# A graph network in four layers: where the turned rows are copied, and when, in layer 3

## The chip, the cores and the metric

The kernel runs on one core of a Trainium2 chip. Its time is what the device takes for one execution, in microseconds (us); a measured time is a median of several executions. Beside it one execution was profiled. The core's engines are named as in the profile: PE (TensorE, matrix products), PEld (its weight loads), DVE (VectorE), ACT (ScalarE), POOL (GpSimd) and SP (SyncE, which here only issues transfers).

## What is computed

A graph of 3327 nodes has 256 features per node (`x`) and a dense adjacency matrix `adj` of 0 and 1. Four layers follow each other, and each ends in `x = layernorm(x + layer(x, adj))`. Layer 0 is an attention by cosine similarity, layer 1 a graph attention, layer 2 an attention with queries, keys and values. Layer 3, which the change concerns, is three graph attentions in a row:

```python
def _gat_layer(h, adj, W, a):
    Wh = h @ W
    f1 = Wh @ a[:F_out]
    f2 = Wh @ a[F_out:]
    e = leaky_relu(f1 + f2.T, 0.01)
    att = softmax(where(adj > 0, e, -9e15), axis=1)
    return elu(att @ Wh)

h = x @ W0
h = _gat_layer(h, adj, W1, a1)
h = _gat_layer(h, adj, W2, a2)
h = _gat_layer(h, adj, W3, a3)
```

All is in 32-bit floating point. The kernel applies a sublayer's attention to its input first and multiplies by `W` afterwards; `W0` is folded into `W1`.

## The kernel before

**Tiles, blocks and steps.** The nodes are padded to 26 tiles of 128 (`NT`). Destination nodes go in 7 blocks (`NB`): blocks 0 to 5 have 512 nodes, block 6 has 256. The main loop (L1552) runs over six sublayers (keys "0", "1", "2", "3a", "3b", "3c"), inside each over the blocks `b`, and inside each block over the 26 source tiles `j`. One turn of the innermost loop is called a step here.

**Weights.** For each step a tile of unnormalised attention weights is needed, 128 source nodes by the 512 nodes of the block. In layer 3, ACT makes `re` from a row of scores `u` (L787; four buffers, tag "a"), and DVE turns `re` into `ft` with the adjacency mask (L800). The main loop asks for the weights several steps ahead of their use (`ahead_of`, L1573 to 1581).

**Products.** Two source tiles and two halves of the block make a 2x2 product by Strassen's method in Winograd's form. DVE builds the sums of weights `qsum` (L871 to 874), four tiles at a time. The sums of the other operand, `tsums`, were stored in memory by `combine` (L830) in the sublayer before and are fetched by SP (L857), one for each pair of steps, into three buffers. `products` (L907) issues 14 products for each pair of steps, so 182 for a block; the trace has two records for each product, since a 32-bit product is done in two passes. Accumulation is in four banks of PSUM, of five.

**The finish of a block.** When a block's last step is done, `finish` (L1093) is started for it. It is a generator, and `advance` (L1457) runs it on to its next `yield` once per step, so its parts are spread over the steps of the next block. At step 22 all that is left of it is run out (L1691). For a block of layer 3 the parts are these:

1. `joined` (L943) on DVE adds the partial products up; `normed` on ACT divides by the row sums and gives `p4`.
2. `turn` (L983): ACT splits the 32-bit numbers of `p4` into 16-bit halves (`planes`, L990, two copies of 128x1024). SP issues a transposing DMA from `planes` to `turned` (L993). After `steps` yields, two copies of 128x1024 (L1000), on DVE, put the halves together as `pT`, the turned rows.
3. `projected(k)` for each of four tiles: two products on PE with `W` (L1230, four passes, to `pproj`), then an exponential on ACT (`elu_e`, L1239) and either a second activation on ACT (`z`, L1242, in 3a and 3b) or an operation of DVE (L1245, in 3c).
4. `activated(k)`, one yield after `projected(k)`: DVE makes the new row (L1254). In 3a and 3b it adds it to a running sum (L1084) and makes the scores for the next sublayer (L719); `combine` follows after the second and the fourth tile. In 3c, statistics, normalisation (L1283) and the output DMAs follow.
5. In 3a and 3b, after three more yields, `rows` (L761): a transposition of the scores on PE (`psr`, L765), a copy on ACT (L767) and a small DMA.

How many steps the DMA is given is set by `turn_steps`; `b == NB - 2` is block 5, whose finish runs in the short block 6:

```python
if L.key == "1":
    return 5 if b == NB - 2 else 3
return (9 if L.key == "3c" else 7) if b == NB - 2 else 4
```

**Order.** The loop gives each operation a place, and buffers give it its waits. The order in which the instructions stand on each engine in the trace is not simply that of the loop: DVE's `joined` is mixed with `qsum`, for example. A planner at build time decides it from the loop's order and from when it thinks inputs are ready.

The buffers of the finish: `planes`, `pT` and `combine`'s `tsum` share the tag "x4k" (two buffers), `p4`, `turned` and 3c's `x4` and `o4` the tag "stage" (four), projections the three PSUM banks of `bank`.

Of the kernel before, what the change touches and what calls it, by code (L numbers as in the profile page):

```python
# [33 lines left out]
def gnn_stack(ctx: ExitStack, tc: tile.TileContext, a: dict, N: int, out: bass.AP):  # L34
# [8 lines left out]
    nc = tc.nc  # L43
    NT = (N + P - 1) // P
    NP = NT * P
    NB = (NP + CH - 1) // CH
# [36 lines left out]
    n = 8  # L83
# [738 lines left out]
    def deep(L):  # L822
        return L.i > 2
# [6 lines left out]
    def combine(key, p, v, e=None):  # L830


        b1, b2 = v[2 * p], v[2 * p + 1]
        b11, b12, b21, b22 = b1[:, H:D], b1[:, :H], b2[:, H:D], b2[:, :H]
        if (key, p) in kept or key == "0":
            t = work.tile([P, 4 * H + 1], F32, tag="tsum", name="tsums", bufs=3)
        else:
            t = work.tile([P, 4 * H + 1], F32, tag="x4k", name="tsum", bufs=2)
        if (key, p) in kept:
            tsums[kept[key, p], p] = t  # L840
        t1, t2, t3, t4 = (t[:, c : c + H] for c in (0, H + 1, 2 * H + 1, 3 * H + 1))
        if e is None:
            nc.gpsimd.memset(t[:, H : H + 1], 1.0)
            nc.vector.tensor_tensor(t1, b12, b11, ALU.subtract)
            nc.vector.tensor_tensor(t3, b22, b12, ALU.subtract)
        else:
            one = t[:, H : H + 1]
            nc.vector.tensor_scalar(one, e[:, :1], 0.0, None, ALU.is_ge)
            nc.vector.scalar_tensor_tensor(t1, b12, one, b11, ALU.mult, ALU.subtract)
            nc.vector.scalar_tensor_tensor(t3, b22, one, b12, ALU.mult, ALU.subtract)  # L850
        nc.vector.tensor_tensor(t2, b22, t1, ALU.subtract)
        nc.vector.tensor_tensor(t4, t2, b21, ALU.subtract)
        nc.sync.dma_start(t_d[key][p], t)
# [126 lines left out]
        return z[:, : 2 * q]  # L980


    def turn(x4, n, out, steps=3):  # L983

        half = "p k (n t) -> p t k n"
        pl = work.tile([P, 4, 2, D], U16, tag="x4k", name="planes", bufs=2)
        for t in range(2):
            nc.scalar.copy(pl[:, :n, t, :], x4[:, :n, :].bitcast(U16).rearrange(half, t=2)[:, t])  # L990
        yield
        tr = work.tile([P, 16, P], U16, tag="stage", name="turned", bufs=4)
        nc.sync.dma_start_transpose(  # L993
            out=tr[:, : 4 * n, :], in_=pl[:, :n].rearrange("p k t n -> p (k t n)")
        )
        for _ in range(steps):
            yield
        trv = tr[:, : 4 * n, :].rearrange("p (k t h) i -> p t k h i", t=2, h=2)
        for t in range(2):
            nc.vector.tensor_copy(out(t), trv[:, t])  # L1000
        yield

    def turn_steps(L, b):

        if L.key == "1":
            return 5 if b == NB - 2 else 3
        return (9 if L.key == "3c" else 7) if b == NB - 2 else 4

# [82 lines left out]
    def finish(L, b, pos):  # L1093
# [4 lines left out]
        n = len(ts_)  # L1098
# [71 lines left out]
        else:  # L1170
# [23 lines left out]
            if L.key in x_d:  # L1194
                x4 = work.tile([P, 4, D], F32, tag="stage", name="x4", bufs=4)
# [8 lines left out]
            if L.key != "2":  # L1204
                pT4 = work.tile([P, 4, 2, P], F32, tag="x4k", name="pT4", bufs=2)
                yield from turn(
                    p4,
                    n,
                    lambda t: pT4[:, :n].bitcast(U16).rearrange(
                        "p k h (i t) -> p t k h i", t=2  # L1210
                    )[:, t],
                    turn_steps(L, b),
                )
                pTs = {k: pT4[:, k] for k in range(n)}
                if L.key == "1" and b < NB - 2:
                    c4 = work.tile([P, 4, D], F32, tag="x4k", name="c4", bufs=2)
                    yield from projected4(pT4, w[L.w], c4)

            def projected(k):


                if L.key == "2":
                    src = p4[:, k, :]
                elif L.key == "1" and b < NB - 2:
                    src = c4[:, k, :]
                else:
                    pm = bank("pproj")
                    pT = pTs.pop(k)
                    for h in range(2):
                        nc.tensor.matmul(  # L1230
                            pm[:, :D],
                            pT[:, h, :],
                            w[L.w][:, h, :],
                            start=(h == 0),
                            stop=(h == 1),
                        )
                    src = pm[:, :D]
                e = work.tile([P, D], F32, tag="elu_e", name="elu_e", bufs=2)
                nc.scalar.activation(e, src, AF.Exp)  # L1239
                if L.hidden:  # L1240
                    y = work.tile([P, D], F32, tag="y", name="z", bufs=6)
                    nc.scalar.activation(y, src, AF.Relu)  # L1242
                else:
                    y = work.tile([P, D], F32, tag="y", name="y", bufs=6)
                    nc.vector.scalar_tensor_tensor(  # L1245
                        y, src, 0.0, xr[k], ALU.max, ALU.add
                    )
                es[k] = e
                ys.append(y)

            def activated(k):
                e, y = es.pop(k), ys[k]
                x = nxt[ts_[k]][:, :D] if L.hidden else y
                nc.vector.scalar_tensor_tensor(x, e, 1.0, y, ALU.min, ALU.add)  # L1254
                if L.hidden:
                    follow([k], {k: x})
                else:
                    stats(k)

            for p in range(n + 2):  # L1260
                if p >= 2:
                    activated(p - 2)
                    if b == NB - 2:
                        yield
                    if L.hidden and p % 2 and b < NB - 1:
                        combine(layers[L.i + 1].key, (ts_[0] + p - 3) // 2, nxt)
                if 1 <= p <= n:
                    projected(p - 1)
                if p > 0:
                    yield  # L1270
        if not L.hidden:
# [29 lines left out]
            if L.key == "1":  # L1301
                yield from turn(
                    o4,
                    n,
                    lambda t: FT[b].bitcast(U16).rearrange(
                        "p h (k i t) -> p t k h i", k=4, t=2
                    )[:, t, :n],
                    4 if b == NB - 2 else 3,
                )
                for k, t in enumerate(ts_):  # L1310
                    pm = bank("pv")
                    for h in range(2):
                        nc.tensor.matmul(
                            pm[:, :D],
                            FT[b][:, h, k * P : (k + 1) * P],
                            w["v"][:, h, :],
                            start=(h == 0),
                            stop=(h == 1),
                        )
                    nc.vector.tensor_tensor(nxt[t][:, :D], pm[:, :D], w["bv"], ALU.add)  # L1320
                    if k % 2:
                        yield
                        if b < NB - 1:
                            combine("2", t // 2, nxt)
                dsts = [nxt[t][:, :D] for t in ts_]
# [146 lines left out]
    steps = [(L, b, j) for L in layers for b in range(NB) for j in range(NT)]  # L1472
# [79 lines left out]
    for s, (L, b, j) in enumerate(steps):  # L1552
# [146 lines left out]
        if j == NT - 1:  # L1699
            if b == 0 and not last:  # L1700
                nl = layers[L.i + 1]
                L.sum = Sum()
                if nl.is_gat:
                    if nl.key == "1":
                        while "row_1" not in w:
                            next(setup)
                    nl.gat = Gat(nl.key)
                    L.gat_next = nl.gat
            if end:
                pending.append(finish_last(pos[1:], xm, 1))  # L1710
            else:
                pending.append(finish(L, b, pos))
            advance()
# [65 lines left out]
```

## Time and profile before

| | |
|---|---|
| median of 3 executions | 2298.59 us (2297.35 to 2298.78) |
| profiled execution | 2297.41 us, of which the span is 2295.6 us |
| layer 3, from its first product to the end | 1372.2 to 2295.6 us of the span |
| busy over the span | PE 98%, PEld 87%, DVE 87%, ACT 53%, POOL 2% |
| DMA | 286.13 MB, mean 125 GB/s |

The products of the blocks of layer 3 start at these times in the span (us):

| sublayer | 0 | 1 | 2 | 3 | 4 | 5 | 6 |
|---|---|---|---|---|---|---|---|
| 3a | 1372.2 | 1418.4 | 1465.7 | 1511.4 | 1558.8 | 1605.3 | 1651.0 |
| 3b | 1677.6 | 1722.4 | 1768.0 | 1813.7 | 1862.4 | 1910.7 | 1956.2 |
| 3c | 1982.8 | 2027.7 | 2072.5 | 2118.0 | 2162.6 | 2207.9 | 2252.4 |

An instruction's record has a start and a length. On PE, DVE and ACT records of instructions that follow each other overlap a little, so the cost of one in a full queue is the distance from its start to the next start. An arrow `<-` behind an idle time names what ended it. Idle time of an engine that isn't the bound costs nothing.

### The profile page before, as it was taken

Reading aid. Unit: us, or ns where it says so; the run is one execution under the profiler, and the core shown is the slowest. Engines: PE = TensorE matmul, PEld = TensorE weight load, DVE = VectorE, ACT = ScalarE, POOL = GpSimd, SP = SyncE. Lnnn points to the kernel's source line nnn. Section 1 sums busy time; section 2 is a strip of 40 time slices with the busy share of each in tenths; the row PEclk is TensorE's granted clock in tenths of the full one; section 3 lists DMA queues with packets and bytes.
Section 4 is the critical chain, followed back from the end, with each engine's and each line's share of the span. In section 5 each row is a group of like instructions: output and inputs, shape, how many; then the busy total and the mean of one; then the engine's idle time right before and its main releaser. Section 6 shows DMA issues by size and latency. Waiting matters only on the chain. (4 is left out here: it accounts for less than half of the span.)

```text
span 2295.6 us, 41529 instructions
## 1 busy us (share of the span) xinstructions
PE 2257.2 (98%) x15183; PEld 2004.7 (87%) x15183; DVE 1998.3 (87%) x5437; ACT 1210.3 (53%) x1982; POOL 49.4 (2%) x196
## 2 busy tenths in 40 slices
PE   9999999999999999999999999999999999999997
PEld 7788888888888877888888899999999999999997
DVE  7789999866777777898898889999899999899996
ACT  4667777764555423223223246555666555655653
POOL 0000001000000000000000000000000000000000
PEclk9999999999999999999999999999999999999999
DMA  8655565523222322132132254444444445355542
GB/s 281 192 178 179 186 195 187 161 84 89 78 72 55 105 61 81 56 100 81 56 99 71 74 171 130 133 136 143 124 129 137 131 134 148 98 152 169 149 122 58
DMA packets 186207, 286.13 MB, mean 125 GB/s; under 512 B 80413, under 2 KB 105492, under 8 KB 181396
## 3 DMA queue, kind: packets, MB, share of 16 engines
q1 hardware_dynamic: 185732, 283.22, 41.2%
q8 instruction: 120, 1.97, 0.4%
q14 instruction: 83, 0.68, 0.1%
q10 hardware_dynamic: 272, 0.26, 0.0%
HBM read 228.21 MB, written 38.44 MB: 116 GB/s over the span
## 5 line engine op out<-in xcount | busy, mean ns | idle before, releaser
L787 ACT ACTIVATE re<-u,nrh,th 128x512 f32<-128x512 f32 (+1 forms) x728 | 539.8, 778 | 343.0 <-DVE ft L800 179.7
L1644 PE MATMUL po<-v,e 128*128 128x257 f32 x1872 | 422.3, 381 | 0.9 <-ACT p L1177 0.8
L1644 PEld LDWEIGHTS po<-v,e 128*128 128x128 f32 x1872 | 352.6, 190 | 60.9 <-issue 9.8
L935 PE MATMUL po<-tsums,qsum 128*128 128x128 f32 (+1 forms) x2520 | 352.8, 275 | 1.4 <-DMA tsums<-t3b_d 0.7
L800 DVE SCALAR_TENSOR_TENSOR ft<-re,rh,mask 128x512 f32<-128x512 f32 x468 | 341.1, 747 | 2.6 <-ACT re L787 2.6
L935 PEld LDWEIGHTS po<-tsums,qsum 128*128 128x128 f32 x2520 | 316.2, 192 | 3.5 <-DVE qsum L873 1.6
L935 PE MATMUL po<-tsums,ssum 128*128 128x128 f32 (+1 forms) x2082 | 293.2, 276 | 4.0 <-DMA tsums<-t3a_d 1.7
L935 PE MATMUL po<-v,ft 128*128 128x129 f32 x1872 | 286.1, 276 | 1.3 <-DVE p L975 0.6
L935 PEld LDWEIGHTS po<-tsums,ssum 128*128 128x128 f32 x2082 | 262.6, 192 | 7.0 <-DVE ssum L885 2.0
L935 PEld LDWEIGHTS po<-v,ft 128*128 128x128 f32 x1872 | 248.2, 192 | 4.0 <-issue 1.8
L935 PEld LDWEIGHTS po<-v,e 128*128 128x128 f32 x1196 | 172.3, 191 | 37.6 <-issue 24.9
L935 PE MATMUL po<-v,e 128*128 128x129 f32 x1196 | 185.1, 275 | 0.0
L800 DVE SCALAR_TENSOR_TENSOR e<-re,rh,mask 128x512 f32<-128x512 f32 (+1 forms) x234 | 149.1, 657 | 38.4 <-PE po L1644 28.4
L524 ACT ACTIVATE ex<-ps,rq 128x512 f32<-128x512 f32 (+1 forms) x183 | 118.9, 652 | 114.7 <-PE ps L511 109.9
L511 PE MATMUL ps<-ft 128*128 128x512 f32 (+1 forms) x364 | 166.9, 564 | 0.0
L496 DVE SCALAR_TENSOR_TENSOR e<-ex,mask 128x512 f32<-128x512 f32 (+1 forms) x182 | 115.8, 650 | 49.0 <-ACT ex L694 27.1
L935 PE MATMUL po<-tsums,ft 128*128 128x128 f32 x936 | 144.2, 275 | 0.0
L525 DVE SCALAR_TENSOR_TENSOR e<-ex,mask 128x512 f32<-128x512 f32 (+1 forms) x183 | 116.8, 644 | 31.1 <-ACT ex L524 30.5
L686 PE MATMUL ps<-gT,ft 128*128 128x512 f32 (+1 forms) x336 | 129.8, 527 | 0.0
L935 PE MATMUL po<-v,qsum 128*128 128x128 f32 x840 | 128.8, 275 | 0.0
L935 PEld LDWEIGHTS po<-tsums,ft 128*128 128x128 f32 x936 | 124.9, 193 | 0.3
L660 ACT ACTIVATE ex<-ex,off 128x512 f32<-128x512 f32 x98 | 67.0, 716 | 101.7 <-DVE ex L676 69.1
(346 smaller groups left out, 3572.8 us busy)
## 6 DMA issues: line engine op xcount, KB each, us to landing
mask<-mask_d SPq DMA_DIRECT2D x30, 1664.0 KB
stage<-in_adj_a SPq DMA_DIRECT2D x78, 512.0 KB
tsums<-t_d SPq DMA_DIRECT2D x152, 256.5 KB
tsums<-t3a_d SPq DMA_DIRECT2D x77, 256.5 KB
tsums<-t3b_d SPq DMA_DIRECT2D x77, 256.5 KB
tsums<-t3c_d SPq DMA_DIRECT2D x77, 256.5 KB
mask_d<-mask SPq DMA_DIRECT2D x6, 1664.0 KB
u<-s_d SPq DMA_DIRECT2D x24, 256.0 KB
```

What stands on the lines that cost most here:

```text
L496: nc.vector.scalar_tensor_tensor(e[:, :wd], t_[:, :wd], 0.0, mask(b, j), ALU.add, ALU.mult)
L511: nc.tensor.matmul(ps[:, :wd], FT[j // 4][:, 0, (j % 4) * P : (j % 4 + 1) * P], FT[b][:, 1, :wd], start=True, stop=True,)
L524: nc.scalar.activation(t_[:, c], ps[:, c], AF.Exp, scale=rq[:, j : j + 1])
L525: nc.vector.scalar_tensor_tensor(e[:, c], t_[:, c], 0.0, mask(b, j)[:, c], ALU.add, ALU.mult)
L660: nc.scalar.activation(x[k], x[k], AF.Exp, bias=off, scale=1.0 / D**0.5)
L686: nc.tensor.matmul(ps[:, :wd], FT[j // 4][:, h, (j % 4) * P : (j % 4 + 1) * P], g[:, h, :wd], start=(h == 0), stop=(h == 1),)
L787: nc.scalar.activation(t_[:, :wd], self.u[b][:, :wd], AF.Relu, bias=self.nrh[:, j : j + 1], scale=self.th[:, j : j + 1],)
L800: nc.vector.scalar_tensor_tensor(e[:, :wd], t_[:, :wd], self.rh[:, j : j + 1], mask(b, j), ALU.add, ALU.mult,)
L935: nc.tensor.matmul(o, x, y, start=(p == 0 and g not in banks[:i]), stop=(p == NT // 2 - 1 and g not in banks[i + 1 :]),)
L1644: nc.tensor.matmul(pos[k], e[:, k * P : (k + 1) * P], V[L.i % 2][i], start=(i == 0), stop=(i == NT - 1),)
```

## The change

In layer 3, for blocks 0 to 4, the turned rows get seven steps where they had four, the two copies to `pT` go from DVE to ACT, two more yields stand between these copies and the first projection, and one more after each of the four activations. Blocks 5 and 6 and the other layers keep their numbers: `turn_steps` still gives block 6 four steps and block 5 seven or nine.

```diff
-    def turn(x4, n, out, steps=3):
+    def turn(x4, n, out, steps=3, copy=nc.vector.tensor_copy):
...
         for t in range(2):
-            nc.vector.tensor_copy(out(t), trv[:, t])
-        yield
+            copy(out(t), trv[:, t])
+        yield
+
+    def early(L, b):
+        return deep(L) and b < NB - 2
 
     def turn_steps(L, b):
 
         if L.key == "1":
             return 5 if b == NB - 2 else 3
-        return (9 if L.key == "3c" else 7) if b == NB - 2 else 4
+        if b == NB - 1:
+            return 4
+        return 9 if L.key == "3c" and b == NB - 2 else 7
...
                     turn_steps(L, b),
+                    nc.scalar.copy if early(L, b) else nc.vector.tensor_copy,
                 )
+                if early(L, b):
+                    yield
+                    yield
                 pTs = {k: pT4[:, k] for k in range(n)}
...
                 if p >= 2:
                     activated(p - 2)
-                    if b == NB - 2:
+                    if b == NB - 2 or early(L, b):
                         yield
```

`deep(L)` is true for 3a, 3b and 3c.

## The prediction

> **What bounds the kernel now.** I first cut layer 3 into its blocks and asked for the busy time of each engine in them. Columns: from:to, length, then busy us (and instructions) of PE, PE's weight load, DVE, ACT, POOL, then granted clock, DMA share, GB/s. Three blocks of sublayer 3b, then two of 3c:
>
> ```profile
> core 0: us, PE busy (x) PEld busy (x) DVE busy (x) ACT busy (x) POOL busy (x), PEclk, DMA share, GB/s
> ...
> 1768.00:1813.70 45.70, 44.95 (x383) 44.00 (x383) 45.36 (x109) 28.24 (x45) 0.20 (x2) 1.00 0.51 142
> 1813.70:1862.40 48.70, 46.43 (x383) 45.14 (x383) 45.76 (x107) 27.39 (x44) 0.20 (x2) 0.96 0.47 133
> 1862.40:1910.70 48.30, 46.00 (x383) 44.92 (x382) 44.71 (x101) 27.17 (x43) 0.20 (x2) 0.96 0.43 114
> ...
> 2118.00:2162.60 44.60, 44.31 (x382) 43.70 (x381) 44.04 (x99) 26.12 (x39) 0.00 (x0) 1.00 0.52 154
> 2162.60:2207.90 45.30, 44.68 (x383) 43.91 (x383) 44.79 (x104) 27.13 (x40) 0.00 (x0) 1.00 0.48 134
> ```
>
> PE and DVE are both nearly full, ACT is at 60%. The same work takes 44.6 us in one block and 48.7 in another, so up to 4 us of a block are stalls. The timeline of the 48.7 us block, where its first projection comes, shows the stall (start, length, instruction, idle before it and releaser):
>
> ```profile
> 1823.45 2.99 SPq L993 DMA_TRANSPOSE turned<-planes  x1
> ...
> 1826.77 0.69 DVE L872 TENSOR_TENSOR qsum<-ft 128x512 f32<-128x512 f32 x1
> ...
> 1829.84 1.37 DVE L1000 COPY pT<-turned 128x1024 uint16<-128x1024 uint16 x2 [2.38 <-issue]
> ...
> 1831.11 0.68 DVE L873 TENSOR_TENSOR qsum<-qsum,ft 128x512 f32<-128x512 f32 x1
> ...
> 1831.27 2.36 PE L1230 MATMUL pproj<-w_l_w,pT 128*128 128x256 f32 x5 [2.23 <-DVE pT L1000]
> ```
>
> The turned rows are late. DVE stands 2.38 us in front of its copies and PE 2.23 us in front of the projection that needs them. The waits of the stretch 1372 to 2295 us confirm it for all blocks (us in total, times, longest):
>
> ```profile
> DVE pT L1000 <- DMA turned<-planes: 13.1, 10, 3.4
> DVE pT L1000 <- issue: 6.2, 4, 2.4
> ...
> PEld pproj L1230 <- DVE pT L1000: 16.0, 15, 2.5
> ...
> PE pproj L1230 <- DVE pT L1000: 12.7, 13, 2.3
> ...
> ACT re L787 <- DVE ft L800: 179.7, 207, 5.7
> ```
>
> The first four lines are this one place; the only other waits of PE in layer 3 that reach 1 us are three at a sublayer's start or end, 1.6 at most. The last line says that ACT, as maker of `re`, mostly waits for DVE: it has time to give.
>
> **What the Trainium skill says.** "Perfetto Trace Analysis", Identifying the Most-Contended Engine: occupancy is a fair measure for Vector and Scalar, matmul busy time is not for Tensor. Here I therefore build PE's floor from start-to-start times. The same page, Tensor Engine Instruction, says ACT and DVE are strict FIFO: what stands behind a waiting copy waits too. The trace agrees: DVE's `qsum` L873 starts only after the copies. "TensorE: Matmul & The Clock Gate", What's actually happening: the PE clock is halved after idleness. The trace shows it after the 2.23 us stall: projection passes then start every 0.43 us, not every 0.217 us, for some 4 us, and the block's mean clock is 0.96. "ScalarE: Activation LUTs", Rules for kernel authors, budgets 0.3 us plus 0.83 ns per element; an estimate of 1.15 us for a 1024-element copy. The trace has 1.036 us for `planes`, same shape and type, same engine; I use that.
>
> **The change, part by part.** It acts on the finish of blocks 0 to 4 in 3a, 3b, 3c, which runs inside the next block: 15 stretches, blocks 1 to 5 of each sublayer. Their lengths now: 3a 47.3+45.7+47.4+46.5+45.7 = 232.6; 3b 45.6+45.7+48.7+48.3+45.5 = 233.8; 3c 44.8+45.5+44.6+45.3+44.5 = 224.7; together 691.1 us.
>
> *Copies leave DVE.* Two per block. Each record is 0.74 us but they overlap: from the first copy's start to the next instruction is 1831.11 − 1829.84 = 1.27 us. 15 × 1.27 = 19 us of DVE work goes, and so does DVE's wait for the rows (I add up 16.8 us in the 15 blocks by the gap before the copies, beyond back-to-back spacing). Summing start-to-start costs, DVE has 44.8 us of work in blocks 1 to 4 on average; after, 43.5.
>
> *Copies arrive on ACT.* Second start 0.94 us after the first, as for `planes`: 1.98 us per block to the next start, 30 us in all. ACT is busy 27 of 45 us, so this costs nothing as long as DVE has `re` tiles left (four buffers). Without that cover it is a stall of DVE, priced below.
>
> *Steps.* A step is half a pair of products, some 1.7 us. Three more before the copies, two more before the first projection, one more after each of four activations: nine. Now the projections belong at steps 6 to 9; after, at 11, 13, 15, 17. The recorded order is not simply that of the steps: PE runs the first three projections together after 65 to 74 products (42 by step), so a planner puts an instruction where it believes its input ready. After the change the first projection should stand after about 84 products, 84 × 2 passes × 0.1116 = 18.7 us into the block. The rows land, by the start of the copies, 13.6 to 17.0 us into the block (15 blocks; five late ones near 16 to 17). Plus 2.0 us on ACT: pT at 15.6 to 19.0. So the PE stall goes in fourteen blocks and is at most 0.3 us in the fifteenth.
>
> *What moves with it.* The last activation goes from step 10 to 18, the score row (transposition on PE, copy on ACT, its DMA) from 14 to 22, where all pending work is run out; for 3c the normalisation and output DMAs end there too. The next finish starts at step 25, so nothing overlaps it. The two `combine` stores move to about steps 15 and 19; on SP they stand ahead of later `tsums` fetches, as now, and those wait for PE's buffers anyway (202 waits, 489.9 us in layer 3, nearly no PE wait for `tsums`). The transposing DMA and the mask fetch are where they were. The x4k buffers of `planes` and `pT` are reused in the same order, with at least six steps between the second store and the next `planes`. Zero for all of these; if the stores do block SP, a late `tsums` fetch costs PE about what it costs elsewhere, 0.7 us at the start of a sublayer, say 10 us over 15 blocks.
>
> *The sum.* PE's floor in a block: 182 products × 2 passes × 0.1116 = 40.6, four projections × 4 passes × 0.217 = 3.5, together 44.1; DVE's 43.5 lies under it. So PE becomes the bound by 0.6 us. The best blocks today are 44.5 and 44.6, so some 0.4 of small waits stay; I take 44.6 in 3c and 44.9 in 3a and 3b, which also have the score row and more DVE work. Gain: 232.6 − 224.5 = 8.1; 233.8 − 224.5 = 9.3; 224.7 − 223.0 = 1.7; 19.1 in all. From it I take 1.5 for the five late blocks (0.3 each), where ACT holds back `re`. The profiled execution took 2297.41 (span 2295.6 and 1.8 around it): 2297.4 − 17.6 = 2279.8. The median shown lies 1.2 above the profiled one, so 2281.
>
> **The rivals.** *ACT's queue becomes the wait (slower).* ACT is strict FIFO, and `re` stands behind the copies. The lead of `re` over `ft`, which I counted, is 0 or 1 at 9 to 11 us into a block (ACT has just done `p` and `planes`), 2 or 3 at 13 and 4 at 15. If the planner puts the copies at 11 us, ACT waits to a mean landing of 15.0, then 2.0 of copies and 0.7 for a `re`: 17.7. DVE, using a `re` each 1.3 to 1.7 us, runs dry about 13.5: a stall of 4.2, and 43.5 + 4.2 = 47.7 against 46.3 now: 12 × 1.4 = 17 us slower, 2316. Break-even is a stall of 2.8, which is ACT reaching the copy near 12.4 us. Against it: PE's projections, planned for some 15 us, put the planned landing near 13.3 us; then six `re` of 0.71 us are out since `planes` ended at 9.1, the lead is 2 or 3, and DVE runs dry near 17 in the bad blocks, not before. Chance 0.12.
>
> *DVE stays the bound (half the gain).* The four activations each make DVE wait for ACT and PE now over eight steps, not four, and 3a's first block leaves DVE behind. If blocks settle at about 45.5 in 3a and 3b and 44.8 in 3c, 691.1 − 455 − 224 = 12; with the late landings and some SP waits, 8: 2290. For it: 3a block 1 has 45.5 of DVE work. Against: 1.3 of relief. Chance 0.12.
>
> *The wait only moves.* PE pauses for `pT` at the new place, since landing is later when PE is faster, or the score row now waits at step 22. Landing follows planes, which follow the block's end, so its distance to PE hardly changes. 2298; chance 0.06.
>
> **How the numbers follow.** Forecast 0.70 (2273 to 2287), half gain 0.12, no change 0.06, slower 0.12. Within 0.2% (4.6 us) is about what a measurement of this kernel can't tell from no change. The low end is every block at its floor, 44.3 and 44.2: 691.1 − 664 = 27, so 2272. The high end is set at 2296, beyond the half gain and short of the last two cases, leaving out less than 0.2. Faster 0.82, same 0.06, slower 0.12.
>
> **What would show it.** In the profile after: `pT` copies on ACT near 1.04 us; no PE wait for pT above 0.5 us; no stretch of clock 0.96 in 3b blocks 3 and 4; those two blocks near 45; DVE idle now before `ft` for lack of PE's progress, not of rows. Wrong if DVE shows waits for ACT `re` over 2 us in most blocks, if PE's first projection stands far from 84 products, or if SP's stores make PE wait for `tsums`.

## The result, and the profile after

The kernel after takes 2297.69 us (median of 22 executions, 2292.4 to 2302.05), the kernel before beside it on the same chip 2299.07 us (22, 2295.08 to 2301.47): a ratio of 0.9992, 95% interval 0.9986 to 0.9999. That is less than 2 us where 17.6 us was forecast. The two profiled executions even stand the other way round, 2298.3 against 2297.41 us. The 15 blocks in which the change acts took 690.4 us in the trace before and 692.1 us in the trace after.

The busy time by stretch for the kernel after, columns as before: block 2 of 3a, blocks 3 and 4 of 3b, block 3 of 3c.

```profile
core 0: us, PE busy (x) PEld busy (x) DVE busy (x) ACT busy (x) POOL busy (x), PEclk, DMA share, GB/s
...
1463.20:1512.20 49.00, 46.38 (x383) 45.59 (x383) 45.63 (x105) 30.30 (x46) 0.20 (x2) 0.97 0.49 148
...
1816.50:1862.70 46.20, 44.59 (x383) 43.84 (x382) 43.57 (x102) 29.63 (x47) 0.20 (x2) 1.00 0.50 141
1862.70:1908.90 46.20, 44.76 (x384) 44.01 (x384) 42.12 (x99) 28.43 (x45) 0.20 (x2) 1.00 0.44 117
...
2118.70:2164.20 45.50, 44.64 (x383) 43.91 (x382) 43.54 (x105) 28.32 (x41) 0.00 (x0) 1.00 0.53 157
```

The two long blocks of 3b went from 48.7 and 48.3 to 46.2 each, at full clock. But others grew: 3a's block 2 from 45.7 to 49.0, at a clock of 0.97, and the 3c block shown from 44.6 to 45.5.

The waits in the stretch that holds the 15 blocks, 1417 to 2254 us (us in total, times, longest), first of DVE in the kernel before:

```profile
DVE pT L1000 <- DMA turned<-planes: 9.7, 9, 2.6
DVE pT L1000 <- issue: 6.2, 4, 2.4
...
DVE v L1254 <- ACT z L1242: 3.2, 4, 1.2
DVE ft L800 <- ACT re L787: 2.6, 2, 1.3
```

Then of DVE, ACT and PE in the kernel after:

```profile
DVE ft L800 <- ACT re L787: 14.2, 8, 2.6
DVE v L1263 <- ACT z L1251: 12.4, 15, 1.4
...
DVE y L1254 <- ACT elu_e L1248: 5.0, 7, 1.1
...
ACT pT L1000 <- DMA turned<-planes: 21.7, 13, 4.2
...
PE po L935 <- ACT re L787: 9.2, 7, 2.4
PE po L935 <- DVE p L975: 3.4, 6, 1.0
PE po L935 <- DVE zs L970: 2.2, 1, 2.2
...
PE pproj L1239 <- DVE pT L1000: 0.9, 2, 0.5
```

PE's wait for `pT`, 12.7 us before, is gone; the 0.9 us left belongs to copies that stayed on DVE. Before, DVE stood 15.9 us in front of its copies. Now ACT stands 21.7 us in front of them, and DVE waits 31.6 us for ACT, where it had waited 5.8. PE stalls at its ordinary products, `po`, instead, mostly in the first microseconds of a block. Where ACT `re` is named as the releaser there, I take the cause to be the banks, as in the timeline below: in 3a's block 3, PE's stall ends at 1513.89, just after DVE's second L970 (1513.71 to 1513.85), which reads one of them.

The timeline of 3a's block 2 (from 1463.2) shows the chain: start, length, instruction, and the idle time before it with what ended it. ACT, DVE, PE, then SP.

```profile
1474.83 2.93 ACT L787 ACTIVATE re<-u,nrh,th 128x512 f32<-128x512 f32 x4
1477.95 0.81 ACT L787 ACTIVATE re<-u,nrh,th 128x512 f32<-128x512 f32 x1 [0.19 <-DVE ft L800]
1482.96 2.54 ACT L1000 COPY pT<-turned 128x1024 uint16<-128x1024 uint16 x2 [4.19 <-DMA turned<-planes]
1485.37 4.34 ACT L787 ACTIVATE re<-u,nrh,th 128x512 f32<-128x512 f32 x6
...
1465.49 0.15 DVE L967 COPY zs<-po 128x2 f32<-128x2 f32 x1
...
1482.90 0.68 DVE L874 TENSOR_TENSOR qsum<-ft,qsum 128x512 f32<-128x512 f32 x1
1486.20 1.46 DVE L800 SCALAR_TENSOR_TENSOR ft<-re,rh,mask 128x512 f32<-128x512 f32 x2 [2.63 <-ACT re L787]
...
1490.27 0.43 DVE L1263 SCALAR_TENSOR_TENSOR v<-elu_e,z 128x256 f32<-128x256 f32 x1 [0.74 <-ACT z L1251]
...
1466.19 1.13 PE L935 MATMUL po<-tsums,qsum 128*128 128x128 f32 x8 [2.23 <-DVE zs L970]
...
1462.88 13.80 SPq L857 DMA_DIRECT2D tsums<-t3a_d  x4
1476.77 2.94 SPq L993 DMA_TRANSPOSE turned<-planes  x1
```

Read it from the bottom. PE is ready for the new block near 1464, but DVE reaches the sums of the old one (L967) only at 1465.5, and those free PE's banks: a stall of 2.23 us. The finish begins late, and SP, which issues in order, still stands at a `tsums` fetch that waits for PE's buffers, so it issues the transposition at 1476.8. The rows land 19.8 us into the block. ACT has waited 4.19 us for them, with nothing behind the copies allowed to pass. The copies and one `re` take until about 1486.2; DVE took its last `re` at 1482.2 and is idle 2.63 us.

For all 15 blocks I made a ledger of DVE and PE: the cost of an instruction is the distance to the next start, its work is the 30th percentile of that distance for its kind, and what exceeds it by over 0.15 us is a wait. It is made from one execution of each kernel, and single executions differ: the time up to the 15 blocks, in which nothing was changed, is 1416.9 to 1420.6 us in the traces of this study without the fifth `re` buffer. In the ledger PE's work is 659.4 us before and after.

| us in 15 blocks | before | after |
|---|---|---|
| length | 690.4 | 692.1 |
| DVE work | 659.1 | 641.0 |
| DVE waits | 28.6 | 46.6 |
| of these for rows (`pT`) | 15.8 | 0 |
| for `re` (`ft`) | at most 0.4 | 14.2 |
| for `elu_e` and `z` (`v`, `y`) | 1.9 | 16.5 |
| PE stalls at projections | 17.3 | 0.3 |
| PE stalls at products (`po`) | 5.2 | 23.2 |

18.1 us of work left DVE, and 18.0 us of waits came. That the two balance is no finding by itself, since work and waits add up to nearly the length, and the length hardly changed; what the ledger shows is where the waits stand. PE lost 17 us of stalls in the middle of the blocks and got 18 us of them back, mostly at the blocks' starts.

### The profile page after: what moved, and what is told of

It reads as the page before. It is cut to its first block, busy times and chain, and to the rows that moved or that the text cites. A ratio compares the mean times of both kernels' runs of the same rounds, so it can differ in the third digit from the quotient of the medians.

```text
span 2296.5 us, 41597 instructions
## 1 busy us (share of the span) xinstructions
PE 2253.7 (98%) x15183; PEld 2004.9 (87%) x15183; DVE 1982.4 (86%) x5407; ACT 1239.4 (54%) x2012; POOL 41.6 (2%) x196
## 3 DMA queue, kind: packets, MB, share of 16 engines
q1 hardware_dynamic: 185732, 283.22, 41.2%
## 4 chain that ended last, share of the span: by engine, by line
PE 75%; DVE 14%; DMA 4%; ACT 4%; issue 2%; POOL 0%; DVEq 0%; SPq 0%; ACTq 0%; POOLq 0%
PE po L935 35%; PE po L1653 16%; PE ps L647 6%; PE ps L511 6%; PE ps L686 5%; DVE ft L800 3%; DMA turned<-planes 2%; PE pproj L1239 2%; ACT re L787 2%; DVE qsum L873 1%; DVE qsum L872 1%; DVE ejunk L719 1%; PE pv L1322 1%; PE pgq L541 1%; DVE qsum L874 1%
## 5 line engine op out<-in xcount | busy, mean ns | idle before, releaser
L935 PE MATMUL po<-tsums,qsum 128*128 128x128 f32 (+1 forms) x2520 | 353.9, 277 | 15.8 <-ACT re L787 9.2
L800 DVE SCALAR_TENSOR_TENSOR ft<-re,rh,mask 128x512 f32<-128x512 f32 x468 | 339.1, 740 | 16.1 <-ACT re L787 14.2
L935 PEld LDWEIGHTS po<-v,ft 128*128 128x128 f32 x1872 | 252.9, 193 | 9.7 <-issue 5.0
L496 DVE SCALAR_TENSOR_TENSOR e<-ex,mask 128x512 f32<-128x512 f32 (+1 forms) x182 | 115.4, 648 | 48.9 <-ACT ex L694 31.6
```

The lines of the kernel that those rows point to most:

```text
L496: nc.vector.scalar_tensor_tensor(e[:, :wd], t_[:, :wd], 0.0, mask(b, j), ALU.add, ALU.mult)
L800: nc.vector.scalar_tensor_tensor(e[:, :wd], t_[:, :wd], self.rh[:, j : j + 1], mask(b, j), ALU.add, ALU.mult,)
L935: nc.tensor.matmul(o, x, y, start=(p == 0 and g not in banks[:i]), stop=(p == NT // 2 - 1 and g not in banks[i + 1 :]),)
```

## The experiments

Four theories stand in the expectations. A: the copies on ACT wait for rows and hold up `re` and the activations, and that costs DVE what it was given. B: the four activations spread over more steps do the harm. C, from the second group on: the finish is late and PE waits for its banks at the block's start wherever the copies are. In the third group A is split: D says that it is ACT's wait for the rows, E that it is ACT's 2.5 us with the copies, wait or no wait.

All runs, with the ledger of their 15 blocks (length, DVE work, DVE waits, PE stalls; all us). Each ratio is to the kernel before on the same chip in the same group.

| run | us | ratio, 95% interval | length | DVE work | DVE waits | PE stalls |
|---|---|---|---|---|---|---|
| e1_copies_on_dve | 2305.78 | 1.0032 (1.0022 to 1.0042) | 699.0 | 656.5 | 38.7 | 25.6 |
| e2_copies_alone | 2304.75 | 1.0029 (1.0019 to 1.0040) | 696.4 | 640.3 | 50.2 | 29.1 |
| e3_no_act_yields | 2297.32 | 0.9995 (0.9988 to 1.0001) | 688.0 | 641.7 | 40.2 | 22.2 |
| e4_copies_on_pool | 2310.24 | 1.0053 (1.0036 to 1.0070) | 699.5 | 638.2 | 57.0 | 29.6 |
| e5_act_copies_later | 2296.60 | 0.9990 (0.9983 to 0.9996) | 688.0 | 640.3 | 41.7 | 21.4 |
| e6_dve_copies_later | 2284.27 | 0.9935 (0.9922 to 0.9947) | 676.1 | 658.0 | 14.9 | 11.4 |
| e7_rows_not_turned | 2283.20 | 0.9930 (0.9915 to 0.9945) | 674.7 | 658.7 | 13.1 | 8.6 |
| e8_five_re_buffers | 2293.09 | 0.9971 (0.9961 to 0.9982) | 683.4 | 640.8 | 37.7 | 16.9 |
| e9_act_later_not_turned | 2286.43 | 0.9952 (0.9937 to 0.9966) | 679.0 | 640.9 | 32.3 | 14.0 |
| e10_act_later_five_re | 2298.09 | 0.9999 (0.9990 to 1.0008) | 687.5 | 641.1 | 41.2 | 21.2 |
| e11_dve_later_act_yields | 2291.95 | 0.9971 (0.9961 to 0.9981) | 681.5 | 655.3 | 22.4 | 14.7 |
| e12_dve_later_five_re | 2285.38 | 0.9943 (0.9928 to 0.9958) | 674.7 | 658.6 | 13.0 | 9.7 |

The kernel before took 2298.13 us in the first group (e1 to e4), 2298.94 in the second (e5 to e8), 2298.46 in the third. Differences in us below are to these.

In e5, e9 and e10 DVE clears one column of `pT` in each of the 15 blocks (see e5). This is left out of DVE's work: by start-to-start distances it would count 9.4 us, but its record lies inside that of the `ft` before it, and an `ft` with the clearing takes 0.66 us to the next start, as an `ft` alone does.

**e1: the steps without the copies.**

```diff
-                    nc.scalar.copy if early(L, b) else nc.vector.tensor_copy,
+                    nc.vector.tensor_copy,
```

> The whole change, but the copies of the turned rows stay on DVE. Theory A (the copies on ACT wait for the rows and hold back the re tiles behind them; DVE runs dry): DVE's waits for re, 14.2 us in layer 3 of the changed kernel, fall under 3 us; DVE takes its 19 us of copies back but no longer waits for rows (16.8 us before); about 2288 us, 10 under the kernel before. Theory B (the four activations, spread over eight steps, each hold DVE until PE and ACT are there: 17 us of waits of v and y): these waits stay, about 2298 us.

7.7 us slower than before, which neither theory expected. Waits of e1, same stretch:

```profile
DVE pT L1000 <- DMA turned<-planes: 25.0, 15, 3.6
...
PE po L935 <- ACT re L787: 5.5, 3, 2.3
PE po L935 <- DVE zs L970: 5.4, 3, 2.1
PE po L935 <- DMA tsums<-t3b_d: 5.1, 4, 2.3
```

Three more steps did not move the copies. I counted DVE's weight instructions (`ft`, `qsum`) between the block's sums and the copies: 13 or 14 in the kernel before with four steps, and 13 or 14 in e1 with seven. PE's projections did move, from 65 to 74 products to 84. So DVE still stands before the rows, longer than before since they land later (copies start 16.8 us into a block, 15.1 before), and PE no longer pauses meanwhile: it reaches the next block 0.7 us before DVE begins the sums, where before DVE was 0.5 us ahead. This is what C describes, though 5.1 us of PE's waits are for fetches of `tsums`; whether it must be so is seen in e6.

**e2: the copies without the steps.** Four steps, and none of the new yields.

```diff
+        if early(L, b):
+            return 4
...
-                if early(L, b):
-                    yield
-                    yield
...
-                    if b == NB - 2 or early(L, b):
+                    if b == NB - 2:
```

> Only the move of the copies to ACT; four steps, no added yields. Theory A: ACT still waits for the rows with re behind it, and PE, whose projection stands after some 66 products, waits for the slower copies as well: slower than before by 10 to 25 us, 2308 to 2323. Theory B: the copies do no harm by themselves, DVE is 19 us lighter: about 2283.

6.6 us slower. Waits of e2:

```profile
PE pproj L1238 <- ACT pT L1000: 19.6, 15, 2.7
...
DVE v L1262 <- ACT z L1250: 18.9, 12, 3.1
```

A's direction, short of its 10 us. PE waits at the projections, by the ledger 24.8 us where it had 17.3 before (a pair of copies takes some 1.1 us more on ACT than on DVE), and then DVE waits for the activations behind them. Each half alone costs 7 us and the two together gain 1. I read it so: on ACT the copies let DVE go on, and later projections take PE out of the wait.

**e3: activations not spread.**

```diff
-                    if b == NB - 2 or early(L, b):
+                    if b == NB - 2:
```

> The change without the yield after each activation. Theory A: little changes, DVE's waits for re stay at 10 us or more: 2294 to 2300. Theory B: the waits of v and y on DVE fall from 17 to under 7 us, and the time to about 2288.

The same as the change: 0.9995 against 0.9992. By the ledger `v` and `y` still wait 11.8 us and `ft` 7.2, less than in the change; but `e`, the weights of the short block 6, waits some 11 us where it waited some 6, for PE. B falls for the changed kernel: the waits that it blames fall by some 5 us and the time does not.

**e4: the copies on POOL**, which has nearly nothing else to do in layer 3.

```diff
-                    nc.scalar.copy if early(L, b) else nc.vector.tensor_copy,
+                    nc.gpsimd.tensor_copy if early(L, b) else nc.vector.tensor_copy,
```

> The whole change, but the copies on POOL, where nothing else of this stretch stands behind them. Theory A: neither DVE nor ACT waits for the rows, DVE is 19 us lighter and not short of re: 2274 to 2284, if a copy on POOL takes under some 2.5 us; if it takes much longer, PE waits for pT by the difference, 15 times. Theory B: the spread activations hold DVE as in the changed kernel: 2290 or more.

12.1 us slower, the worst of all, though neither DVE nor ACT waits for rows any more. The copies by tile (minimum, median and maximum in ns), and e4's timeline while two of them run:

```profile
L1000 POOL COPY pT<-turned x30: 1427/1784/3157, 1436.0 to 2233.0; 128x1024 uint16<-128x1024 uint16 x30
```

```profile
2094.01 3.42 POOL L1000 COPY pT<-turned 128x1024 uint16<-128x1024 uint16 x2 [46.37 <-DMA turned<-planes]
...
2093.80 2.43 DVE L800 SCALAR_TENSOR_TENSOR ft<-re,rh,mask 128x512 f32<-128x512 f32 x2
2096.16 1.77 DVE L871 TENSOR_TENSOR qsum<-ft 128x512 f32<-128x512 f32 x1
2097.85 0.68 DVE L872 TENSOR_TENSOR qsum<-ft 128x512 f32<-128x512 f32 x1
```

DVE's own instructions are stretched without any wait: a pair of `ft` takes 2.43 us (1.4 elsewhere), a `qsum` 1.77 (0.68). The ledger counts these as waits of `ft` and `qsum`, 32.3 us. So e4 cannot tell the theories apart, though B's 2290 or more was met; it shows another cost.

**e5: copies on ACT, but later.** Ten steps, one yield after `turn`, activations not spread. To give the copies a place in DVE's order as well, DVE clears one column of `pT` first, so ACT's copies can't come before DVE is there.

```diff
+        if gate is not None:
+            nc.vector.memset(gate, 0.0)
         for t in range(2):
             copy(out(t), trv[:, t])
...
+        if early(L, b):
+            return 10
...
+                    pT4[:, 0, 0, :1] if early(L, b) else None,
                 )
                 if early(L, b):
                     yield
-                    yield
...
-                    if b == NB - 2 or early(L, b):
+                    if b == NB - 2:
```

> Copies on ACT, but ten steps after the transposition is issued, with a one-column write of DVE ahead of them that the copies must wait for (so that they can't be placed earlier in ACT's order: eight or nine re tiles ahead of them in 3a and 3b, five or six before), one more yield before the projection and none after activations. Theory A (copies stand too early in ACT's order, wait there for the rows with re behind them, and DVE, which sets the time, runs dry): ACT's wait for rows falls from 24 us to under 5 in the 15 blocks, DVE's waits for re under 4; 2278 to 2288 us. Theory C (a late finish makes DVE add up the next block late, so that PE waits for its banks at the block's start whatever the copies do): PE's stalls before its products stay at 20 us or more, and the time at 2295 or more.

2.3 us faster than before. A's range is missed, and C's expectation comes true, with 20.3 us of PE's stalls at its products. Waits of e5:

```profile
DVE v L1267 <- ACT z L1255: 15.2, 11, 3.4
DVE ft L800 <- ACT re L787: 9.0, 8, 1.3
...
ACT pT L1002 <- DMA turned<-planes: 8.7, 7, 1.7
```

ACT's wait for rows falls from 21.7 to 8.7 us and the time hardly moves, so the loss does not follow from the length of this wait alone (steps and spreading differ too). In the first two or three blocks of each sublayer the clearing put 8 or 9 `re` between `planes` and the copies, in the later ones only 5 or 6, as in the change.

**e6: copies on DVE, later.** e5 without the clearing, with `nc.vector.tensor_copy` for all.

```diff
+        if early(L, b):
+            return 10
...
-                    nc.scalar.copy if early(L, b) else nc.vector.tensor_copy,
+                    nc.vector.tensor_copy,
                 )
                 if early(L, b):
                     yield
-                    yield
...
-                    if b == NB - 2 or early(L, b):
+                    if b == NB - 2:
```

> Copies on DVE, ten steps, one more yield before the projection, none after activations; they stand 15 to 20 operations of weights after the block's sums, where they stood 13 or 14 both with four and with seven steps. Theory A: DVE's wait for rows, 16 us before and 25 in the first experiment, falls under 5: 2282 to 2290. Theory C: PE's stalls at block starts eat it: 2296 or more.

14.7 us faster than before, the best complete kernel of the study. With ten steps the count of DVE instructions before the copies is 15 to 20, no longer 13 or 14. DVE's waits in e6, then its timeline in 3a's block 4:

```profile
DVE pT L1000 <- DMA turned<-planes: 3.9, 4, 1.8
DVE ft L800 <- ACT re L787: 2.6, 2, 1.3
DVE v L1264 <- ACT z L1252: 2.3, 4, 1.2
```

```profile
1572.40 1.36 DVE L1000 COPY pT<-turned 128x1024 uint16<-128x1024 uint16 x2
```

The copies start with no wait before them. DVE has all of its work, 658.0 us, and waits 14.9 instead of 28.6. PE's stalls halve with it, though its first projection stands later still, 22.7 us into a block. So C falls: a later finish by itself does not make PE wait at the block's start; I take DVE being behind to do it, since in e6 it begins the sums 0.2 us ahead of PE's first product. Steps and yields are those of e5. The engine of the copies, with the clearing that costs DVE nothing, makes the whole difference of 12.3 us: on ACT the copies are not free.

**e7: nothing to wait for.** The kernel before, in which the copies of these blocks read `planes`, where they took `turned`; the rows are not turned there, and nobody waits for the DMA.

```diff
+        if flat:
+            trv = pl[:, :n].rearrange("p k t (h i) -> p t k h i", h=2)
```

> The kernel before, but in layer 3, blocks 0 to 4, the copies read the untransposed planes; the transposing DMA is still issued, nothing waits for it (this leaves out the turning of the rows). It measures what the wait for rows is worth. Theory A: DVE's 16 us and PE's 17 us before the projection go: 2280 to 2286. If the wait only moves, as with theory C: 2294 or more.

15.7 us faster than before. This is what rows without a wait are worth, and not quite the price of the wait alone: the planner, with no DMA to wait for, also put the copies earlier, 10.0 us into a block and 6 to 8 weight instructions behind the sums. e6 gets 14.7 us with the rows turned.

**e8: the change with five `re` buffers** where it had four (other small buffers give up the room).

```diff
-            t_ = work.tile([P, CH], F32, tag="a", name="re", bufs=4)
+            t_ = work.tile([P, CH], F32, tag="a", name="re", bufs=5)
...
-                    y = work.tile([P, D], F32, tag="y", name="z", bufs=6)
+                    y = work.tile([P, D], F32, tag="y", name="z", bufs=5)
```

> The changed kernel with five buffers for re and not four (one buffer less for y, and one row shares another buffer, to make room). Theory A: DVE has one more tile in hand when ACT waits, some 1.3 us in each of the blocks where it ran dry: its waits for re fall from 14 us to under 8, 2290 to 2294. Theory C: no effect, 2296 to 2299.

5.9 us faster than before, so some 4.5 us better than the change by the two differences. Waits of e8:

```profile
DVE v L1263 <- ACT z L1251: 16.4, 17, 1.4
...
DVE ft L800 <- ACT re L787: 4.3, 5, 1.3
```

The order of instructions is nearly that of the change. One more tile of lead takes 10 us from the `ft` waits, while ACT still waits 20.0 us for rows. `v` keeps its wait: no `re` buffer helps an activation behind the copies.

**e9: e5 with copies from `planes`.** The order of e5; rows not turned, no wait for the DMA.

```diff
+        if gate is not None:
+            trv = pl[:, :n].rearrange("p k t (h i) -> p t k h i", h=2)
```

> The fifth experiment (copies on ACT, late in its order), but the copies read the untransposed planes, so ACT never waits for rows (this leaves out the turning of the rows in layer 3, blocks 0 to 4); the order of the instructions is the same. Theory D (the wait for rows on ACT is the harm): the time falls to 2284 us or less, as with the copies late on DVE. Theory E (2.5 us of copies on ACT, between re tiles and the activations of the projections, are harm enough: DVE waits for re and for z even so): 2291 us or more.

12.0 us faster than before, where e5 gained 2.3; it falls between D's range and E's. On ACT and DVE the instructions of the 15 blocks stand in the same order as in e5's trace, one for one, so 9.7 us of e5's loss is ACT waiting for rows (D). What still separates e9 from e6 is 2.7 us, with intervals that overlap. It isn't the clearing; ACT's own time (E) is what is left to explain it. DVE has 17 us less work than in e6 and 17 us more waits, for `z` above all:

```profile
DVE v L1268 <- ACT z L1256: 13.3, 10, 3.1
...
DVE ft L800 <- ACT re L787: 2.6, 2, 1.3
```

`ft` is back at its value before, and `v` isn't, at a small price: with no wait for rows left, freeing DVE of the copies gains nothing over e6.

**e10: e5 with the buffers of e8.**

> The fifth experiment with five buffers for re. Theory D: the waits for rows remain, little changes, 2293 to 2297. Theory E: one more re tile covers about half of the copies' 2.5 us; DVE's waits for re and z fall from 24 us to some 12: 2284 to 2290.

No gain over e5 (0.9999 against 0.9990), a miss: I had thought that lead and a later place add up. `ft` waits fall to 3.0 us, but the wait for `z` grows from 15.2 to 18.7.

**e11: e6 with activations spread.**

```diff
-                    if b == NB - 2:
+                    if b == NB - 2 or early(L, b):
```

> The sixth experiment (copies on DVE, ten steps) with the yield after each activation put back. If the spread of the activations were harmful by itself (theory B), 2292 us or more; if not, within 3 us of the sixth experiment, 2281 to 2287.

6.5 us faster than before, so 8 us worse than e6. Waits of e11:

```profile
DVE pT L1000 <- DMA turned<-planes: 9.5, 6, 2.1
DVE v L1264 <- ACT z L1252: 4.9, 6, 1.4
```

The experiment isn't clean: in four of 3c's five blocks its copies again stood 13 or 14 instructions after the sums. But the traces divide the loss. The five blocks of 3a take 225.8 us and those of 3b 225.2, where e6 has 226.6 and 226.2; those of 3c take 230.8 against 223.7, and what follows them 46.8 against 43.3. So the spreading costs nothing in 3a and 3b, though PE newly waits 3.7 us there for the score row (`psr`). In 3c the place of the copies and the spreading are not told apart.

**e12: e6 with the buffers of e8.**

> The sixth experiment with five buffers for re. DVE waited for re only 2 to 4 us there, so with copies on DVE the fifth buffer should give no more than 3 us: 2281 to 2286. If it gives 8 or more, the gain of the fifth buffer in the changed kernel was not about ACT's copies.

Nothing over e6 (0.9943 against 0.9935, intervals overlap). The fifth `re` buffer gained time in the order of the change alone (e8), and with later copies on neither engine (e10, e12).

## Why the prediction was wrong

The forecast of 2281 us failed, and 2297.69 lies outside its range. Its steps in their order:

- *Copies leave DVE*: right. 18.1 us of DVE work left by the ledger, 19 was said, and the 15.8 us wait for rows went too.
- *Copies arrive on ACT*: **the step that failed.** It set their cost at nothing "as long as DVE has `re` tiles left". The size was off: a copy takes 1.346 us, not the 1.036 of `planes`, so two cost some 2.4 us, not 1.98. More than that, the cover was priced for ACT's *work*, with 1.5 us for the late rows, at the landing times of before. The wait for rows, which blocked DVE, now blocked ACT, for 21.7 us, and behind it stood DVE's next `re` and, soon after, the `elu_e` and `z` that DVE's `v` and `y` need. By a count of both queues, ACT is mostly 0 or 1 `re` ahead of DVE at 18 to 21 us into a block. The runs show the cost: with e5's steps, copies on ACT in place of DVE lose 12.3 us (e6), and 9.7 of these are ACT's wait for rows (e9, same order). In the order of the change itself, one more `re` tile of lead gains some 4.5 us (e8); no run takes the wait for rows out of that order.
- *Steps*: right for PE. The first projection stands at 84 products, as said (20.6 us into a block and not 18.7, for PE stalls ahead of it), and PE's stall for `pT` went. Not seen was that the landing would move too: copies started 15.1 us into a block before and 16.5 after. The finish starts later, as DVE is behind PE at the block's start (sums begin 0.8 us after PE's first product; before, 0.5 us ahead of it). "Landing follows planes, which follow the block's end" was right; that the block's end for DVE and for PE part from each other was missed.
- *What moves with it*: zero was right for the stores as such, and PE's waits for `tsums` stayed small (0.8 us is the largest group in the stretch of the 15 blocks). But on SP the transposition itself stands behind a `tsums` fetch, as the timeline of 3a's block 2 shows; how much of the 1.4 us later landing is that, no run separates.
- *The sum*: the two floors were right (659.4 / 15 = 44.0 for PE, 44.1 said; 641.0 / 15 = 42.7 for DVE, 43.5 said). "PE becomes the bound by 0.6 us" compared work with work and left some 0.4 for waits. Measured, a block is 46.1 us: PE's 44.0 of work with 1.6 of stalls, DVE's 42.7 with 3.1 of waits. Such sums name no bound; the waits do. DVE waits for ACT, and PE, at the block's start, for DVE's sums to free its banks.

Of the rivals, *ACT's queue becomes the wait* had the mechanism. Its sizes were off: it had the copies placed early, at 11 us, and `ft` waiting 4.2 us in twelve blocks. They stood behind five or six `re`, as the forecast had argued when it set the rival aside, and `ft` waited 14.2 us in all; `v` and `y`, which the rival left out, added as much again. With the waits for rows that went set against them, DVE's waits grew by 18.0 / 15 = 1.2 us a block, for 1.2 us of work saved. *DVE stays the bound* named the engine but not the reason: e3 shows that the spread activations, which it blamed, do nothing here. *The wait only moves* has the right time by another way: PE does not wait for `pT` at the new place.

Of the signs listed in advance, the absence of PE waits for `pT` and the full clock in 3b's blocks 3 and 4 came true; copies near 1.04 us and blocks near 45 did not. The sign set for failure, waits for `re` over 2 us in most blocks, was too coarse: they were 8 with 2.6 as the longest, and waits of 1 us for `z` did as much.

What was true all along is that there are some 15 us to be won from the wait for rows (e7). In these runs giving the wait to an engine with idle time did not win them; placing the copies where the rows have landed, on DVE as before, did (e6, 0.9935). Whether ACT would do as well with turned rows that have always landed wasn't tried; e9, where they aren't turned, comes near.

## What to carry to other kernels

A wait in an in-order queue can cost whatever stands behind it, so before moving an instruction with its wait to an idler engine, look at what that engine feeds within the next few microseconds, and to whom. If the engine that is relieved lives on the other's output with few tiles of lead, move the instruction in time before moving it in space. And where a planner sets the order, count instructions in each queue of the trace: a yield more in the loop may shift one engine's part and leave the other's where it was.

## What the runs showed of the hardware

- A copy of 128x1024 16-bit elements on ACT takes 1.036 us from `p` to `planes` and 1.346 us from `turned` to `pT`; read from `planes` instead (e9) it is 1.337 us. So it isn't the DMA's target that makes it slow; I take it to be the interleaved writing of `pT`, which was not tried alone. The Trainium skill, "ScalarE: Activation LUTs", Rules for kernel authors, budgets some 0.3 us for an activation whose bias comes through a pointer and 0.83 ns for each element. From this I estimate 1.15 us for 1024 elements: one copy is below, the other above. DVE's records of the `pT` copy are 0.74 us.
- POOL takes 1.43 to 3.16 us for the same copy, and while it runs, DVE's 32-bit instructions take up to 2.6 times their length (1.77 against 0.68 us). Here an idle POOL was not free help beside a full DVE.
- A stall of PE can cost more than itself, also at a new place: the 49.0 us block after, with its stall of 2.23 us, shows a clock of 0.97, where before the two 3b blocks with stalls of 2.2 and 2.3 us showed 0.96. The length of the stall does not decide it alone: a block of e8 with a stall of 1.87 us (at 1608) shows 0.96, a block of e5 with one of 2.65 us (at 1908) 1.00.
